# The MLP's second matrix as two nested levels of seven products, its operands formed ahead on GpSimd and streamed from DRAM

## The chip, the cores and the metric

One core of a Trainium2 chip. The metric is the device time of one execution in microseconds; the time before is the median of three runs. Engines by their short names: PE is TensorE (PEld its weight loads), DVE is VectorE, ACT is ScalarE, POOL is GpSimd, SP issues the DMAs. Everything is float32. P = 128 partitions, F = 512 features.

## The reference, cut to what matters

Four sequences of 1024 rows with 512 features run through a graph attention (L0) and then through a conditioned transformer block (L1).

```python
# L0: v is (4, 1024, 512); 20 neighbours, 16 heads of 32; twice (d = 0, 1)
self_feat = concat([v, q_exp]) @ W_self.T + b_self
w   = softmax(where(mask, qh . kh / sqrt(32), NEG) + label_bias)      # over 20 neighbours
out = einsum(w, kv) through Wout per head;  x = v + relu(self_feat + out_0 + out_1)

# L1: c = cond, six vectors per sequence from silu(c) @ W_mod + b_mod
x = x + g_msa * (attention(modulate(layernorm(x))) @ W_out + b_out)   # 16 heads of 64
x = x + g_mlp * (gelu(modulate(layernorm(x)) @ W1 + b1) @ W2 + b2)    # 512 -> 2048 -> 512
```

W2 has 2048 rows and 512 columns. The product `gelu(...) @ W2` over all 4096 rows is what the change touches.

## The kernel before

Order on every engine is the order in which the program emits instructions (`tc.manual_schedule()`); each engine and the queue of SP run their instructions in that order, each waiting for its own inputs.

**Graph attention.** A loop over steps `s` from -4 to 33 handles 32 tiles of 128 rows, software-pipelined: step `s` has the scores of tile `s`, the softmax of tile `s` (`g_soft1` on DVE, `g_soft2` on GpSimd, `g_soft3` on DVE, `g_soft4` = Exp on ACT, `g_soft5` on DVE and GpSimd), the transposes of the weights of tile `s-1` on PE (`g_weightsT`), the mask work of later tiles (`g_mask1` on GpSimd, `g_mask2` on DVE) and loads four tiles ahead. GpSimd's order in a step is: `t + add` (g_soft2), cast and product of the mask (g_mask1), `wts` = weights times reciprocal sum (g_soft5).

**Products in sevens.** A product of two 2x2 block matrices is formed with seven block products instead of eight. `sums_a` and `sums_b` form the sums of blocks (four subtractions or additions each; one of them in place). `seven` issues the products in the order a, c, b, a2, b2, d, b3 into four PSUM banks ma, mb, mc, md, with small steps between them: ACT copies bank a to bank b; ACT keeps c in SBUF (`s5`); DVE writes bank d as b + s5 (`start_d`) ahead of b2; DVE forms the last quarter as b + s5 (`last`) ahead of b3; each finished quarter (i, j) goes to `done`. `with_four` runs them in that order.

**The MLP** comes last, in blocks of 512 rows (`k` = 0 to 7, VB = 4 tiles). For each block:

- The up phase: for `p` = 0 to 3 (2 and 3 for the first block) seven products of W1 with the transposed, modulated rows `hT`; `gelu` on ACT writes the hidden values into `hs[p]` as four groups of blocks, and `up_sums(p)` on DVE forms the hidden values' sums in `hx[p]` (four operations of 128x512).
- The down phase: seven products with W2, each of 2 x 16 matmuls with the hidden values as stationary and 256 columns of W2 as moving operand. W2 lies in SBUF (`w2s`, 4 MB, loaded once) with three sums of its quarters (`w2x`), formed by DVE once.
- `between()`, emitted after the first product of the down phase: `norm_turn` transposes the next block's four normalised tiles (`xl`) in 32x32 blocks on DVE, alternately into `tx["mlp"][:, 5]` and a buffer `s`, and four DMAs per tile carry each result into `hT`; with every second block the gates are spread again (`spread`); then the block's own rows are loaded from `x2d` into `rows2`, whose four buffers (tag `xl`) are those of the tiles just transposed; and GpSimd adds `bias2` to the four of them.
- `modulated()`, after the fourth product: ACT scales and shifts `hT` (`norm_mod`), GpSimd forms the next up phase's sums (`mlp_rows`, four operations of 128x512).
- `dn_done`: each quarter is multiplied with the gate and added to `rows2` on DVE; finished rows are stored to `out`.

The SP queue carries, in the order of emission, the rows for the next block (`norm_load`), the 16 transposing DMAs, the four row loads and the stores.

Of the kernel before, what the change touches and what calls it, by code (L numbers as in the profile page):

```python
# [12 lines left out]
F32 = mybir.dt.float32  # L13
# [28 lines left out]
def cond_block_kernel(  # L42
# [86 lines left out]
    x2d = [tc.dram_tile([P, F], F32, name=f"x2d{i}") for i in range(NTA)]  # L129


    with ExitStack() as gctx:
# [273 lines left out]
        qp = ctx.enter_context(tc.tile_pool(name="qp", bufs=1, side="right", reuse_waits="tile"))  # L406
        xp = ctx.enter_context(tc.tile_pool(name="xp", bufs=1, side="right", reuse_waits="tile"))
# [293 lines left out]
        def up_sums(p):  # L701
            h = [hs[p][:, 2 * k : 2 * k + 2, :] for k in range(4)]
            sums_a(nc.vector, [hx[p][:, k] for k in range(3)], *h)


# [205 lines left out]

        for s in range(-4, NTA + 2):
            do(g_load, s + 4)
# [16 lines left out]
            do(g_mask1, s + 3)  # L930
            do(g_soft3, s)
# [30 lines left out]
            if s == 31:  # L962
                weight_sums(nc.gpsimd, ("v", 0, 0), wv[0, 0], home_ex)
            if s == 25:
                load_qk(0, 0)
                load_v(0, 0)
                load_qk(0, 1)
# [618 lines left out]
    with ExitStack() as mctx:  # L1586
# [12 lines left out]
        w2s = [mp2.tile([P, 4, F], F32, name=f"w2_{k}") for k in range(4)]  # L1599
        for k in (0, 2, 1, 3):  # L1600
            nc.sync.dma_start(w2s[k], w2[k * F : (k + 1) * F, :].rearrange("(c p) f -> p c f", p=P))
        w2x = [mp2.tile([P, 3, 4, HB], F32, name=f"w2x{k}") for k in range(2)]
        for p in range(4):
            hx[p] = mp2.tile([P, 3, 2, HB], F32, name=f"hx{p}")
# [8 lines left out]
        def dn_lhs(which, t, c):  # L1613
            p, q = divmod(c, 2)
            rows = slice(t * P, (t + 1) * P)
            at = {4: 0, 5: 1, 2: 2}.get(which)
            if at is not None:
                return hx[p][:, at, q, rows]
            return hs[p][:, 2 * {0: 0, 1: 1, 6: 2, 3: 3}[which] + q, rows]

        def dn_rhs(which, t, c):
            k, r = divmod(c, 4)
            at = {4: 0, 5: 1, 3: 2}.get(which)
            if at is not None:
                return w2x[k][:, at, r, :]
            h, f = {0: (0, 0), 1: (1, 0), 2: (1, 1), 6: (0, 1)}[which]
            return w2s[2 * h + k][:, r, f * HB : (f + 1) * HB]
# [141 lines left out]
```

## Time and profile before

| what | us |
|---|---|
| median of three runs (lowest to highest) | 3020.31 (3020.05 to 3021.0) |
| the profiled execution | 3032.2 |
| its span, first to last instruction | 3030.2 |
| graph attention, first to last scores (`pa`) | 73.5 to 403.8 of the span |
| attention of L1, first scores (`psc`) to last values (`pav`) | 418.8 to 2263.3 |
| first down phase starts | 2299.7 |
| last product of the last down phase starts | 3018.2 |

The trace's times count from the span's first instruction. The page shows busy time by engine; the windows table shows busy time of each engine in a stretch, then the granted TensorE clock (1.00 is full speed), the mean busy share of the DMA engines and the rate in GB/s; a line of the timeline shows start, duration, engine, line, operation, out<-in, shape and count, and in brackets how long the engine had been idle and who released it. "SPq" lines are the issuing of DMAs, not their transfer.

### The profile page before, as it was taken

What the parts mean: (1) busy time and instruction counts of PE and PEld (TensorE: products, weight loads), DVE (VectorE), ACT (ScalarE), POOL (GpSimd) and SP (SyncE); (2) the same over time, 40 slices, a digit from 0 to 9 for tenths busy, and PEclk for the clock granted to TensorE, in tenths of its full rate; (3) what the DMA queues carried; (4) which work ended last, traced back from release to release, by engine and by line L of the source; (5) the groups of instructions that cost most, each with busy time, mean ns of one, the idle gap of its engine ahead of it and who ended that gap; (6) DMA issues with size and microseconds to landing.
All of it is one profiled execution on the core that took longest, in us unless ns stands there. A gap on an engine that the chain in (4) does not pass through costs nothing.

```text
span 3030.2 us, 41832 instructions
## 1 busy us (share of the span) xinstructions
PE 2995.2 (99%) x15205; PEld 1969.9 (65%) x15205; DVE 2018.4 (67%) x2852; ACT 1441.5 (48%) x2380; POOL 1339.4 (44%) x922
## 2 busy tenths in 40 slices
PE   9999999999999999999999999999999999999999
PEld 6666665565555555555565555555568888888888
DVE  3788867787878877878887878887865332233222
ACT  2344456555755555755555755556641322222211
POOL 1444456555665655665665575664641101110110
PEclk8999999999999999999999999999999999999999
DMA  6343437776877776867776877876764212212020
GB/s 193 118 131 117 136 99 188 167 173 157 204 169 191 191 175 151 209 167 194 190 173 151 206 168 184 198 175 153 190 177 127 49 32 60 56 35 56 29 63 14
DMA packets 341833, 425.25 MB, mean 140 GB/s; under 512 B 88105, under 2 KB 160229, under 8 KB 341629
## 3 DMA queue, kind: packets, MB, share of 16 engines
q1 hardware_dynamic: 341392, 422.37, 55.2%
q8 instruction: 122, 2.00, 0.3%
q14 instruction: 83, 0.67, 0.1%
q10 hardware_dynamic: 236, 0.20, 0.0%
HBM read 120.93 MB, written 25.76 MB: 48 GB/s over the span
## 4 chain that ended last, share of the span: by engine, by line
PE 81%; DVE 7%; POOL 3%; issue 3%; DMA 3%; ACT 2%; SPq 2%; POOLq 0%; DVEq 0%; ACTq 0%
PE q L571 18%; PE psc L1193 14%; PE pav L1101 13%; PE pu L1176 6%; PE mbd L571 5%; PE mbu L571 5%; PE mad L571 4%; PE mau L571 3%; PE mdd L571 2%; PE mcd L571 2%; PE mdu L571 2%; PE mcu L571 2%; DVE mx L1204 1%; DMA wT<-wd 1%; POOL t L780 1%
## 5 line engine op out<-in xcount | busy, mean ns | idle before, releaser
L1219 POOL TENSOR_SCALAR w<-w,sm 128x1024 f32<-128x1024 f32 x256 | 727.8, 2843 | 705.7 <-DVE sm L1215 692.8
L1210 ACT ACTIVATE w<-psc,mx 128x1024 f32<-128x1024 f32 x512 | 570.2, 1114 | 642.8 <-DVE mx L1204 641.6
L1228 DVE STREAM_TRANSPOSE wd<-w 128x1024 f32<-128x1024 f32 x512 | 632.2, 1235 | 110.4 <-ACT w L1217 99.2
L1204 DVE TENSOR_REDUCE mx<-psc 128x1 f32<-128x1024 f32 x512 | 599.3, 1210 | 80.6 <-PE psc L1193 77.4
L1193 PE MATMUL psc<-kT,qT 64*128 64x512 f32 x2048 | 528.0, 615 | 3.6 <-ACT kT L1061 1.4
L1101 PE MATMUL pav<-wT,v 128*64 128x256 f32 x4096 | 482.3, 383 | 2.3 <-DMA wT<-wd 2.0
L1101 PEld LDWEIGHTS pav<-wT,v 128*64 128x64 f32 x4096 | 292.7, 137 | 228.3 <-issue 87.2
L1193 PEld LDWEIGHTS psc<-kT,qT 64*128 64x128 f32 x2048 | 200.2, 186 | 224.0 <-issue 151.4
L1680 POOL TENSOR_TENSOR x<-x,tx 128x512 f32<-128x512 f32 x32 | 39.9, 1279 | 616.9 <-DMA x<-x2d 616.9
L1217 ACT ACTIVATE w<-w,sm 128x1024 f32<-128x1024 f32 x256 | 291.0, 1137 | 0.0
L1185 DVE TENSOR_TENSOR xr<-pu,xr 128x512 f32<-128x512 f32 x210 | 143.6, 684 | 79.7 <-PE pu L1176 79.5
L571 PE MATMUL q<-hT,wqk 128*128 128x512 f32 (+1 forms) x396 | 181.2, 581 | 1.0 <-DVE q L585 1.0
L757 PE MATMUL pa<-kp,sfT 128*128 128x320 f32 x512 | 143.5, 433 | 1.4 <-ACT sfT L732 1.4
L593 ACT COPY mbu<-mau 128x512 f32<-128x512 f32 x30 | 17.1, 570 | 238.9 <-PE mau L571 238.9
L571 PEld LDWEIGHTS q<-hT,wqk 128*128 128x128 f32 x396 | 74.7, 190 | 80.9 <-issue 78.3
L571 PE MATMUL q<-tx,ex 128*128 128x512 f32 (+1 forms) x264 | 123.5, 591 | 1.6 <-POOL tx L656 1.6
L757 PEld LDWEIGHTS pa<-kp,sfT 128*128 128x128 f32 x512 | 94.8, 190 | 38.2 <-ACT sfT L732 1.9
L717 PE MATMUL pf<-wx,xT 128*128 128x512 f32 x256 | 116.0, 597 | 0.0
L571 PE MATMUL mad<-w,hs 128*128 128x256 f32 x512 | 113.1, 379 | 0.0
L571 PEld LDWEIGHTS mad<-w,hs 128*128 128x128 f32 x512 | 97.3, 190 | 13.2
L1176 PE MATMUL pu<-wout,oT 128*128 128x256 f32 x360 | 98.4, 396 | 4.6 <-DVE xr L1185 3.9
L1176 PEld LDWEIGHTS pu<-wout,oT 128*128 128x128 f32 x360 | 62.5, 189 | 59.1 <-issue 31.2
(308 smaller groups left out, 4576.5 us busy)
## 6 DMA issues: line engine op xcount, KB each, us to landing
wT<-wd SPq DMA_DIRECT2D x1024, 256.0 KB
wqk<-in_w_qkv SPq DMA_DIRECT2D x64, 256.0 KB
xT<-in_xt SPq DMA_DIRECT2D x32, 256.0 KB
xs<-in_x SPq DMA_DIRECT2D x32, 256.0 KB
x1d<-xs SPq DMA_DIRECT2D x32, 256.0 KB
xl<-x1d SPq DMA_DIRECT2D x32, 256.0 KB
wv<-in_w_qkv SPq DMA_DIRECT2D x32, 256.0 KB
xr<-x1d SPq DMA_DIRECT2D x32, 256.0 KB
```

The costliest lines, as they stand in the source:

```text
L571: nc.tensor.matmul(t[:, q * width : (q + 1) * width], lhsT=lhs(which, q, k), rhs=rhs(which, q, k), start=(fresh and q == 0 and k == 0), st ...
L717: nc.tensor.matmul(pfs[i], lhsT=xT[i][:, c, :], rhs=wx[:, c, :], start=False, stop=(c == FC - 1), skip_group_check=True,)
L757: nc.tensor.matmul(pas[i][:, n, :HF], lhsT=sfT2[i][:, c, :], rhs=kp[:, b, c, n * HF : (n + 1) * HF], start=False, stop=(c == FC - 1), skip ...
L1101: nc.tensor.matmul(po[j * D : (j + 1) * D, :], lhsT=vt[b, g][:, m, p * P + j * D : p * P + (j + 1) * D], rhs=w[:, j, :, m, :], start=(m == 0),
L1176: nc.tensor.matmul(pu[0][:, q * HB : (q + 1) * HB], lhsT=a[:, q * P : (q + 1) * P], rhs=r, start=(bool(fresh) and q == 0), stop=True, skip ...
L1185: nc.vector.tensor_tensor(o, pu[0].rearrange("p (r f) -> p r f", r=2), o, ALU.add)
L1193: nc.tensor.matmul(sc[j][:, n * F : (n + 1) * F], lhsT=qT[b, gp][q, t * P : (t + 1) * P], rhs=kT[b, gp][q, n * F : (n + 1) * F], start=Tru ...
L1204: nc.vector.tensor_reduce(mx, sc, axis=AX.X, op=ALU.max, negate=True)
L1210: nc.scalar.activation(w, sc, AF.Exp, bias=mx, accum_out=sm)
L1217: nc.scalar.mul(w, w, sm)
L1219: nc.gpsimd.tensor_scalar(w, w, sm, None, ALU.mult)
L1228: nc.vector.transpose(wd[j][:, :, at, :], wn.pop((b, gp, t, j)).rearrange("p (m k) -> p m k", k=U))
```

## The change

W2 is applied as seven products, each of which is again formed by seven: 49 products. For each outer product (`g` counts them, 7 to a block, in the order `ORD` = 0, 4, 1, 5, 6, 2, 3) the stationary operands are 128x128 pieces of the hidden values or sums of them, and the moving operands are 128 columns of W2 or sums of its pieces; an inner product is 4 matmuls.

- **W2's 49 operands** are formed in the graph attention: in four rounds `r` of seven steps (s = -1 to 26) SP loads a quarter of W2 (1 MB) into `w2g` at the end of the round's first step, GpSimd forms the sums in the other six steps (`w2_sum`; two of 128x512 in each of two steps, then one of 128x896 in each of four), emitted between `g_mask1` and `g_soft3`, and SP stores the quarter's 49 pieces (3.2 MB) to `w2d` in DRAM at the end of the last. The buffer takes the place of the pools `qp` and `xp`, which are opened from step 27 on.
- **In the MLP** a ring of three buffers `w2r` takes one outer product's operands (1.84 MB) at a time: `load_w2(g + 2)` is emitted at the start of each outer product, ahead of `between()`.
- **The hidden values' inner sums** (`inner_sums`, four operations of 128x256 for each half `n`) go into `hy[g % 2]`: half 0 on DVE, half 1 on GpSimd, for the next outer product while the present one runs; those of the first outer product of a block and half of the second's are formed by DVE in the up phase.
- `up_sums` loses its fourth operation, which becomes `up_sums4`, run by DVE during the third outer product.
- `inner` has `seven`'s order on the first 128 columns of the four banks, alternating between two sets of banks; a finished quarter goes to one of the accumulators `du`, `d5`, `dv` (ACT copies for outer products 0 and 4, DVE additions for the others).
- `between()` is emitted at the start of the second outer product, without the spreading of the gates, which moves to the start of the down phase; `modulated()` is emitted at the start of the fifth; `finish` multiplies with the gate on DVE and adds to the rows on GpSimd (the last quarter's on DVE).
- The host hands W2 over in another order of its pieces.

```diff
+    w2d = tc.dram_tile([P, 4, 7, 7 * P], F32, name="w2d")
...
-        qp = ctx.enter_context(tc.tile_pool(name="qp", bufs=1, side="right", reuse_waits="tile"))
-        xp = ctx.enter_context(tc.tile_pool(name="xp", bufs=1, side="right", reuse_waits="tile"))
+        gctx2 = ExitStack()
+        tp = gctx2.enter_context(tc.tile_pool(name="tp", bufs=1, side="right", reuse_waits="tile"))
+        w2g = tp.tile([P, 7, 7, P], F32, name="w2g")
...
         def up_sums(p):
-            h = [hs[p][:, 2 * k : 2 * k + 2, :] for k in range(4)]
-            sums_a(nc.vector, [hx[p][:, k] for k in range(3)], *h)
+            a11, _, a21, a22 = (hs[p][:, 2 * k : 2 * k + 2, :] for k in range(4))
+            o1, o2 = (hx[k][:, p] for k in range(2))
+            nc.vector.tensor_tensor(o1, a21, a22, ALU.add)
+            nc.vector.tensor_tensor(o2, o1, a11, ALU.subtract)
+            nc.vector.tensor_tensor(a21, a11, a21, ALU.subtract)
+        def up_sums4(p):
+            nc.vector.tensor_tensor(hx[0][:, p], hs[p][:, 2:4, :], hx[1][:, p], ALU.subtract)
...
+        def w2_load(r):
+            nc.sync.dma_start(w2g[:, :4, :4, :], w2[r])
+        def w2_store(r):
+            nc.sync.dma_start(w2d[:, r], w2g.rearrange("p j i f -> p j (i f)"))
+        def w2_sum(level, n):
+            def at(k):
+                return w2g[:, k, :4, :] if level == 0 else w2g[:, :, k, :]
+            o, i, j = ((4, 1, 0), (5, 3, 4), (1, 3, 1), (6, 2, 5))[n]
+            nc.gpsimd.tensor_tensor(at(o), at(i), at(j), ALU.subtract)
...
         for s in range(-4, NTA + 2):
+            r2, turn2 = divmod(s + 1, 7)
...
             do(g_mask1, s + 3)
+            if 0 <= r2 < 4 and turn2 > 0:
+                for n in ((), (0, 1), (2, 3), (0,), (1,), (2,), (3,))[turn2]:
+                    w2_sum(0 if turn2 < 3 else 1, n)
             do(g_soft3, s)
...
+            if 0 <= r2 < 4 and turn2 == 0:
+                w2_load(r2)
+            if 0 <= r2 < 4 and turn2 == 6:
+                w2_store(r2)
...
-        w2s = [mp2.tile([P, 4, F], F32, name=f"w2_{k}") for k in range(4)]
-        for k in (0, 2, 1, 3):
-            nc.sync.dma_start(w2s[k], w2[k * F : (k + 1) * F, :].rearrange("(c p) f -> p c f", p=P))
-        w2x = [mp2.tile([P, 3, 4, HB], F32, name=f"w2x{k}") for k in range(2)]
+        w2r = [mp2.tile([P, 4, 7, P], F32, name=f"w2r{k}") for k in range(3)]
+        hy = [mp2.tile([P, 4, 2, 2, P], F32, name=f"hy{n}") for n in range(2)]
+        ORD = (0, 4, 1, 5, 6, 2, 3)
+        def load_w2(g):
+            if g < 7 * NB2:
+                at = PLACE[ORD[g % 7]]
+                nc.sync.dma_start(
+                    w2r[g % 3].rearrange("p r i f -> p r (i f)"), w2d[:, :, at]
+                )
...
+        def inner_sums(e, g, n):
+            j = ORD[g % 7]
+            lo, hi = rows_at(j, n), rows_at(j, n + 2)
+            a11, a12, a21, a22 = lo[:, :, :P], hi[:, :, :P], lo[:, :, P:], hi[:, :, P:]
+            o1, o2, o4, o3 = (hy[g % 2][:, k, n] for k in range(4))
+            return [... for o_, x_, y_, op in (
+                    (o1, a21, a22, ALU.add), (o3, a11, a21, ALU.subtract),
+                    (o2, o1, a11, ALU.subtract), (o4, a12, o2, ALU.subtract))]
+        def inner(g, banks, done, room):
...
+            a, b, c, d = (banks[n][:, :P] for n in ("ma", "mb", "mc", "md"))
+            return (
+                (lambda: product(a, 0, True), lambda: nc.scalar.copy(b, a)),
+                (lambda: product(c, 4, True), lambda: nc.scalar.copy(s5, c)),
+                (lambda: product(b, 5), lambda: nc.vector.tensor_tensor(d, b, s5, ALU.add)),
+                (lambda: product(a, 1), lambda: done(0, 0, a)),
+                (lambda: product(b, 6), last),
+                (lambda: product(d, 2), lambda: done(0, 1, d)),
+                (lambda: product(b, 3), lambda: done(1, 0, b)),
+            )
...
+                    if p == 3 and n in (2, 4):
+                        for f in inner_sums(nc.vector, 7 * k, n // 2 - 1):
+                            f()
+                    if p == 3 and n == 2:
+                        for f in inner_sums(nc.gpsimd, 7 * k + 1, 0):
+                            f()
+                if k > 0 or p == 3:
                     up_sums(p)
+                if p == 3:
+                    for f in inner_sums(nc.vector, 7 * k + 1, 1):
+                        f()
...
+            def finish(i, j, y, e=nc.gpsimd):
                 g = gate2[:, j * HB : (j + 1) * HB].unsqueeze(1).to_broadcast([P, 2, HB])
+                nc.vector.tensor_tensor(y, y, g, ALU.mult)
                 for n in range(2):
                     o = rows2[2 * i + n][:, j * HB : (j + 1) * HB]
+                    e.tensor_tensor(o, o, y[:, n], ALU.add)
...
+            for n, which in enumerate(ORD):
+                g = 7 * k + n
+                load_w2(g + 2)
+                if n == 1:
                     between()
+                behind = []
+                if 0 < n < 6:
+                    behind += inner_sums(nc.vector, g + 1, 0)
+                    for f in inner_sums(nc.gpsimd, g + 1, 1):
+                        f()
+                if n == 2:
+                    behind += [lambda p=p: up_sums4(p) for p in range(4)]
+                if n == 3:
+                    behind.append(lambda: finish(0, 0, dv))
+                if n == 4:
+                    nc.gpsimd.tensor_tensor(dv, du, d5, ALU.add)
+                    if nxt < NB2:
+                        modulated()
+                if n == 5:
+                    behind.append(lambda: nc.vector.tensor_tensor(d5, du, d5, ALU.add))
+                if n == 6:
+                    behind += [lambda: finish(0, 1, dv), lambda: finish(1, 1, d5)]
+                done, room = sink(which)
+                steps = inner(g, (dn_banks, up_banks)[n % 2], done, room)
+                for m, (f, after) in enumerate(steps):
+                    f()
+                    after()
+                    for _ in range(-(-len(behind) // (7 - m))):
+                        behind.pop(0)()
+            finish(1, 0, du, nc.vector)
```

## The prediction

> **What bounds the kernel now.** First the page's busy times, then the windows table over one pair of MLP phases, then the timeline of one down phase.
>
> ```profile
> PE 2995.2 (99%) x15205; PEld 1969.9 (65%) x15205; DVE 2018.4 (67%) x2852; ACT 1441.5 (48%) x2380; POOL 1339.4 (44%) x922
> ...
> 2589.98:2638.32 48.34, 48.34 (x225) 42.56 (x224) 10.20 (x19) 4.92 (x8) 9.90 (x8) 1.00 0.25 55
> 2638.32:2686.67 48.35, 48.35 (x225) 42.56 (x224) 17.27 (x28) 17.47 (x38) 0.00 (x0) 1.00 0.10 33
> ```
>
> A down phase (first row: W2 for 512 rows) and an up phase (second row: W1) last 48.35 us each, TensorE without a gap, every other engine mostly idle. There are eight down phases. So TensorE bounds this stage, through the number and width of its matmuls; the others wait at no cost.
>
> ```profile
> 2589.98 7.07 PE L571 MATMUL mad<-w,hs 128*128 128x256 f32 x32
> 2591.86 0.70 DVE L465 STREAM_TRANSPOSE tx<-xl 128x512 f32<-128x512 f32 x1
> 2592.66 2.65 SPq L471 DMA_DIRECT2D hT<-tx  x4
> 2596.88 7.07 PE L571 MATMUL mcd<-w2x,hx 128*128 128x256 f32 x32
> 2597.21 0.71 DVE L465 STREAM_TRANSPOSE tx<-xl 128x512 f32<-128x512 f32 x1 [4.05 <-DMA hT<-tx]
> 2604.50 2.04 SPq L1678 DMA_DIRECT2D x<-x2d  x4
> 2607.39 4.96 POOL L1680 TENSOR_TENSOR x<-x,tx 128x512 f32<-128x512 f32 x4 [83.46 <-DMA x<-x2d]
> 2612.29 1.27 POOL L550 TENSOR_TENSOR tx<-hT 128x512 f32<-128x512 f32 x1
> 2618.60 0.76 DVE L1695 TENSOR_TENSOR x<-x,s 128x256 f32<-128x256 f32 x2
> ```
>
> The reader is to see a long side chain inside the phase: DVE transposes the next block's rows (the third waits 4.05 us for the first one's DMA), SP issues 16 transposing DMAs of 0.66 us, then four row loads, and only then, 17.4 us after the phase began, can GpSimd add the bias to the rows. Today nobody waits for that.
>
> **The change on TensorE.** A product of 32 matmuls of 256 columns takes 6.907 us (2596.88 - 2589.98 = 6.90), 0.216 each. The new phase has 49 products of 4 matmuls of 128 columns.
>
> ```profile
> 416.61 1.28 PE L818 MATMUL po<-vb,wT 128*128 128x128 f32 x10
> ```
>
> Ten of that width take 1.28, and one alone 0.27 (the timeline's row at 414.78): (1.28-0.27)/9 = 0.112 us. 196 x 0.112 = 21.95 us, against 48.35: 26.4 us less a phase if TensorE stayed the bound. I think it doesn't.
>
> **What it now waits for.** I follow a middle phase, t = 0 where TensorE enters it.
>
> Group 0. Before it DVE has up_sums (three adds ending at 1.25) and, new, four 128x256 inner sums at a pitch of 0.34-0.42 (1.45): to 2.7. The product "d" needs DVE's start_d, so group 0 ends near 4.45 and the first transpose starts at 3.95 (before: 1.9).
>
> Row loads. SP's queue now has the 1.84 MB load of group 3's operand ahead of the 16 transposing DMAs; it waits for group 0 to free the buffer.
>
> ```profile
> 2283.00:2290.00 7.00, 7.00 (x34) 6.17 (x33) 5.68 (x9) 3.23 (x8) 0.00 (x0) 1.00 1.05 392
> ```
>
> At the 392 GB/s of the largest loads it takes 4.7 us, from about 6 to 10.7, and the DMAs behind it on the same queue drain after it. So the third transpose starts at about 13.6, not 9.0 (13.6 = 10.7 + 1.9 of data + 1.0 of completion); 5.5 us of issuing follow, then the loads at 19.2, landing 2.9 later as before: R = 22. If the load delays nothing R = 18; if the queue drains slower, 25.
>
> GpSimd's queue. Between the row adds and the next group's operands there is no way round: half of the inner sums of groups 2 to 6 stand behind the four row adds, in order. From R: row adds 4.95; five times four 128x256 operations,
>
> ```profile
> L545 POOL TENSOR_TENSOR osum<-oT,osum 128x256 f32<-128x256 f32 x30 | 21.9, 728 | 0.0
> ```
>
> 2.85 each time at a pitch of 0.70 = 14.25; two 128x256 adds of the first quarter 1.45 (ahead of group 5's sums); dv = du + d5 1.25; mlp_rows 5.0 (both ahead of group 6's sums, which are the last). Sum 26.9, if nothing disturbs it.
>
> Disturbance. DVE and GpSimd hinder one another where both work from SBUF:
>
> ```profile
> 2336.23 1.71 POOL L550 TENSOR_TENSOR hT<-hT 128x512 f32<-128x512 f32 x1
> 2336.92 2.71 DVE L1695 TENSOR_TENSOR x<-x,s 128x256 f32<-128x256 f32 x2
> ```
>
> The pair that took 0.76 alone takes 2.71 beside GpSimd, and GpSimd's 1.27 becomes 1.71. In that stretch DVE has about 13 inner sums (4.4), four up_sums4 (2.4), single 128x128 adds (0.8), three gate products (1.8) and one sum (0.6): 10 us. I charge half, 5, plus 1 for GpSimd's wait on the gate product: 6 (none to 12). The Trainium skill (SBUF — State Buffer, "Who interferes with whom") says that an operation of DVE with two SBUF inputs and one of GpSimd that reads SBUF exclude each other for a whole instruction, "the other fully blocks"; by that all 10 would count, and the sum below would be 7 x 5 = 35 us longer.
>
> After group 6's last sums two products remain: 1 us, or 3 at half clock (1 to 4). TensorE idles 8 us at the third transpose and about 10 more until R + 5.7, and idle time costs clock:
>
> ```profile
> 12.00:17.00 5.00, 3.22 (x29) 3.03 (x28) 1.50 (x5) 2.34 (x3) 0.00 (x0) 1.00 1.01 352
> ...
> 27.00:32.00 5.00, 5.00 (x17) 3.21 (x17) 1.13 (x3) 0.91 (x2) 0.00 (x0) 0.50 1.06 344
> ```
>
> After gaps of about 2 us at 12-17 the granted clock was 0.50 in all three stretches from 17 to 32, some 15 us of interrupted work. I take 3 us there, and 1.7 us at the start of the up phase (half of 3.4 us of work; none to 2). The skill's clock-gate page (TensorE: Matmul & The Clock Gate, Part 1) lets the clock return after about 3.4 us of busy time; by that the last term would be 1 and the sum 14 us shorter.
>
> Phase: 22 + 26.9 + 6 + 3 = 58, and 1.7 later, against 48.35: **+11.3**. Seven phases: +79. By the bounds 18 + 26.9 + 0 + 1 + 0 = 46 (-2.4, or -17 in all) to 25 + 26.9 + 12 + 4 + 2 = 70 (+21.6, or +151).
>
> Last phase: no transposes, no mlp_rows. Row loads go right behind group 3's load, R = 12.5; 12.5 + 21.9 + 6 + 3 = 43.4: **-5** (-14 to +1). First phase: the DVE sums that form W2's operands go (eight of 1.22 us) with TensorE not waiting for them; its new inner sums precede the last product's add: +1 (0 to 3).
>
> Streaming, 56 loads x 4.7 us: three are ahead when a phase starts; groups 5 and 6 are loaded from the ends of groups 2 and 3 (R + 11, R + 18) and needed at R + 23 and R + 33. Nothing; that cover is the GpSimd chain, and without it see the rivals.
>
> **The graph attention.** 24 steps of about 10.5 us get GpSimd sums between its last mask operation and the softmax's scaling: 8 steps two of 128x512 (1.27), 16 steps one of 896 columns (2.47 x 896/1024 = 2.15).
>
> ```profile
> 252.38 0.82 DVE L788 TENSOR_TENSOR t<-t,mx 128x640 f32<-128x640 f32 x1
> 255.47 1.27 POOL L799 TENSOR_TENSOR wts<-t,sm 128x640 f32<-128x640 f32 x1 [3.91 <-DVE sm L797]
> 256.80 0.77 PE L806 MATMUL pt<-ident,wts 128*128 128x128 f32 x5 [0.74 <-POOL wts L799]
> ```
>
> GpSimd's 3.91 us gap would take them, but DVE's subtraction (two SBUF inputs) starts 0.8 us into it. A 2.15 us sum from 251.6, where the last mask operation ends, holds it until 253.75: 1.37 late; two short ones, 0.45. Exp, sum, scaling and TensorE's transposes follow, and TensorE already waits there. 16 x 1.37 + 8 x 0.45 = 25.5; DVE has about 0.45 us a step to spare (15.1 us idle before its 32 first multiplies), 24 x 0.45 = 10.8. Between 14.7 and 25.5 I take **+18** (0 if the sums slip behind the subtraction, 30 with GpSimd's second sum late too). Four stores of 3.2 MB (8.2 us) sit ahead of the next mask loads on SP's queue; those are used some 13 us after issue (202.2 to 215 and later): nothing, a few us if missed.
>
> **Sum.** 79 - 5 + 1 + 18 = +93. The profiled execution took 3032.2 us, its span 3030.2; the runs' median is 3020.3, to which I add the difference: **3113 us**.
>
> **Rivals.**
> A. GpSimd's chain at its floor: R = 18 and DVE's sums fitting into GpSimd's pauses, 46 us a phase. 7 x -2.4 - 14 + 1 + 0..18 = -30 to -12: about 3000. This ends on the other side; it decides where R + 26.9 + the rest falls below 46, two under today. For it: every GpSimd duration is measured. Against: SP's extra load, and the rows of 2.71. Chance 0.10 (0.06 faster, 0.02 equal, 0.02 slower).
> B. TensorE stays the bound (21.95 + 1.3 for group 0: -25 a phase, -200, 2838), or the stream bounds it: 4.45 + 1.3 + 4 x 4.7 + 3.4 = 28, -20 a phase, 2880 with the attention's 18. It needs row adds that don't stand before the sums. 0.04.
> C. The stream is late besides: at half the rate of the big loads (9.4 us each) group 6 lands at R + 18 + 2 + 2 x 9.4 = 61 and the phase ends at 65: with 1.7, +18, 7 x 18 + 19 = +145 and more with a colder clock: 3165 to 3230. For it: rows of 3.5 KB with a stride that no row here shows. 0.10, half of it above my range.
> D. My sum, 3040 to 3165: 0.76.
>
> A measurement of this kernel tells some 0.2% (6 us) from no change. Faster 0.10, same 0.02, slower 0.88. Range **3035 to 3175**: it leaves out B, most of A and half of C.
>
> **What would show it.** In the changed profile: a gap of 8 us or so in TensorE before group 1's "b" products and of some 10 before group 2's; GpSimd's row adds at about 22 us and its busy time unbroken from there to the end of mlp_rows; granted clock under 1 in the down phases; down phases of 55 to 62 us and up phases of 49 to 50; PE waiting for "wts" in the attention, its last step some 18 us later. I am wrong if TensorE is dense in the down phases, or if GpSimd's row adds come before 16 us.

## The result, and the profile after

| | median of the runs, us | lowest to highest | runs |
|---|---|---|---|
| before | 3020.31 | 3017.8 to 3021.34 | 5 |
| after | 3192.75 | 3187.04 to 3197.91 | 5 |

The ratio is 1.0571, with a 95% interval of 1.0555 to 1.0587: 172 us slower. The forecast was 3113 us, with a range of 3035 to 3175. The direction was right, the size was not.

The page of the changed kernel first: busy time, share of the span and instructions of TensorE, VectorE, ScalarE and GpSimd, and the granted clock in forty slices.

```profile
PE 3014.1 (94%) x16549; PEld 2026.9 (63%) x16549; DVE 2213.3 (69%) x3316; ACT 1474.4 (46%) x2524; POOL 1602.2 (50%) x1202
...
PEclk9999999999999999999999999999988988988989
```

TensorE was at 99% and is at 94%, and the last quarter of the span, the MLP, no longer has the full clock. The windows table over one middle block of the MLP (a stretch, then busy time of PE, PEld, DVE, ACT and POOL, the granted clock, the DMA share, GB/s): the first row is a down phase, the second the up phase behind it.

```profile
2555.30:2623.16 67.86, 51.04 (x393) 50.47 (x392) 32.04 (x72) 8.97 (x26) 31.66 (x35) 0.85 0.61 189
2623.16:2671.51 48.35, 48.35 (x226) 42.57 (x225) 20.37 (x34) 17.46 (x38) 3.96 (x4) 1.00 0.26 89
```

The up phase takes 48.35 us as before. The down phase takes 67.86 instead of 48.34. The number in the bracket behind PEld is the most useful one on the page: 392 weight loads for a phase that has 196 matmuls in the program. The timeline of the same phase, TensorE, VectorE and GpSimd (start, duration, operation, shape, records, idle time before and who ended it):

```profile
2562.44 1.06 PE L1694 MATMUL mcu<-w2r,hy 128*128 128x128 f32 x8
2563.33 1.06 PE L1694 MATMUL mbu<-w2r,hy 128*128 128x128 f32 x8
...
2571.77 0.71 DVE L467 STREAM_TRANSPOSE tx<-xl 128x512 f32<-128x512 f32 x1 [10.31 <-DMA hT<-tx]
...
2573.98 2.08 PE L1694 MATMUL mbu<-w2r,hy 128*128 128x128 f32 x8 [8.70 <-DVE mdu L1711]
2575.85 1.92 PE L1694 MATMUL mdu<-w2r,hy 128*128 128x128 f32 x8
2577.56 1.56 PE L1694 MATMUL mbu<-w2r,hx 128*128 128x128 f32 x8
2578.96 1.06 PE L1694 MATMUL mad<-w2r,hs 128*128 128x128 f32 x8
...
2581.06 4.91 POOL L1763 TENSOR_TENSOR x<-x,tx 128x512 f32<-128x512 f32 x4 [33.65 <-DMA x<-x2d]
...
2586.71 1.22 PE L1694 MATMUL mcd<-w2r,hy 128*128 128x128 f32 x4 [6.25 <-POOL hy L1672]
...
2606.31 0.29 DVE L1785 TENSOR_TENSOR du<-mad,du 128x128 f32<-128x128 f32 x1 [1.84 <-POOL dv L1817]
2608.03 1.16 PE L1694 MATMUL mbd<-w2r,hs 128*128 128x128 f32 x8 [1.87 <-DVE s L1705]
```

Three things are to be seen. An inner product, four matmuls in the program, is eight records, and products follow one another every 0.893 us (2563.33 - 2562.44 = 0.89); 49 of them are 43.76 us of TensorE's own work. TensorE stands still three times: for VectorE, which is stuck in front of the third transpose; for GpSimd, whose sums stand behind the row adds; and near the end for VectorE again, which has itself waited 1.84 us for GpSimd's `dv = du + d5`. And behind a wait the products start 1.7 to 1.9 us apart (half clock: 0.50 granted from 2573.98 to 2578.50); behind the first it lasts some 4.6 us (the last of the three slow products took 1.40 instead of 0.89). So 67.86 = 43.76 of work + 16.8 of these three waits + 7.3, nearly all of it half clock.

The whole by the two traces: the first down phase starts at 2325.4 instead of 2299.7 (+25.6); the seven phases with a block behind them take 472.1 us instead of 7 x 48.35 (+133.7); the last takes 54.9 (+6.5). The sum, 165.8, is the difference of the spans but for rounding (3196.1 - 3030.2 = 165.9).

The first of these three numbers is too small. The traced execution of the kernel before granted TensorE only 0.50 of its clock from 17 to 32 us, where all twelve other traces of this case show 1.00; its first mask addition (`t + add`) in the attention comes at 79.0 us, in the others at 68.4 to 70.4, and it took 12 us more than its median. Counted from that addition, the first down phase starts after 2220.7 us in the kernel before and after 2257.0 in the changed one: 36 us later, not 25.6. By the medians it is 172.4 - 133.7 - 6.5 = 32.

### The profile page after: what moved, and what is told of

Read it like the earlier page. It is cut to its first block, busy times and chain, and to the rows that moved or that the text cites. A ratio compares the mean times of both kernels' runs of the same rounds, so it can differ in the third digit from the quotient of the medians.

```text
span 3196.1 us, 45619 instructions
## 1 busy us (share of the span) xinstructions
PE 3014.1 (94%) x16549; PEld 2026.9 (63%) x16549; DVE 2213.3 (69%) x3316; ACT 1474.4 (46%) x2524; POOL 1602.2 (50%) x1202
## 3 DMA queue, kind: packets, MB, share of 16 engines
q1 hardware_dynamic: 371536, 537.98, 62.6%
## 4 chain that ended last, share of the span: by engine, by line
PE 74%; DVE 8%; DMA 5%; POOL 4%; issue 3%; ACT 3%; SPq 3%; POOLq 0%; DVEq 0%; ACTq 0%
PE q L573 17%; PE psc L1226 14%; PE pav L1134 13%; PE pu L1209 5%; PE mbu L573 5%; PE mau L573 3%; PE mbd L1694 3%; SPq L473 2%; PE mdu L573 2%; PE mcu L573 2%; DVE mx L1237 1%; PE mad L1694 1%; ACT w L1243 1%; PE mbu L1694 1%; DMA hT<-tx 1%
## 5 line engine op out<-in xcount | busy, mean ns | idle before, releaser
L1672 POOL TENSOR_TENSOR hy<-hx 128x256 f32<-128x256 f32 x48 | 43.5, 925 | 317.0 <-PE mbu L573 267.7
L1694 PE MATMUL mbu<-w2r,hy 128*128 128x128 f32 x384 | 59.1, 303 | 59.1 <-DVE mdu L1711 59.1
L1243 ACT ACTIVATION_READ_ACCUMULATOR w<-psc,mx 128x1 f32 x512 | 98.6, 193 | 0.0
```

Source lines behind the costliest of these rows:

```text
L1243: nc.scalar.activation(w, sc, AF.Exp, bias=mx, accum_out=sm)
L1694: nc.tensor.matmul(t, lhsT=lhs(which, *divmod(k, 2)), rhs=w2r[g % 3][:, k, PLACE[which], :], start=(fresh and k == 0), stop=(k == 3), skip ...
```

## The experiments

Three questions stood: what is lost ahead of the MLP, what the MLP's waits hang on, and whether my sum failed only in TensorE's own work.

**Attention without the sums.** `w2_sum` is not issued, and the buffer is cleared once, so that W2's sums are left out of the computation.

```diff
         w2g = tp.tile([P, 7, 7, P], F32, name="w2g")
+        nc.gpsimd.memset(w2g, 0.0)
...
-            if 0 <= r2 < 4 and turn2 > 0:
-                for n in ((), (0, 1), (2, 3), (0,), (1,), (2,), (3,))[turn2]:
-                    w2_sum(0 if turn2 < 3 else 1, n)
```

> Leaves out the 24 steps of GpSimd sums that form W2's operands in the graph attention (the array is cleared once instead; its loads and stores and the whole MLP stay), so the output is not the reference's. Theory: GpSimd's sums hold DVE's subtraction, and the loads and stores cost nothing; the first weighted attention then starts near 445 us again (467.1 in the changed kernel, 445.1 before), and the whole is 22 to 25 us shorter: 3168 to 3171. Rival, the four stores of 3.2 MB and loads on SP's queue delay the masks: at most 8 us comes back, 3185 or more.

Measured: 3169.51 us (3169.31 to 3170.54), 23.2 less than the changed kernel. So much do the sums cost, and it is what the theory gave. But they are not all of the loss. The first weighted values come at 443.1 us, and the 445.1 of the kernel before belong to the execution that began 10 us late: counted from the first mask addition, the first down phase starts after 2230.6 us without the sums and after 2220.7 before. Of these 9.9 us, 6.25 lie in one step, behind the first store of 3.2 MB. Without the sums:

```profile
129.31 0.43 SPq L924 DMA_DIRECT2D w2d<-w2g  x1
130.29 1.06 SPq L158 DMA_DIRECT2D xs<-in_x  x1
141.02 0.63 ACT L176 ACTIVATE xs<-xs 128x512 f32<-128x512 f32 x1 [3.48 <-DMA xs<-in_x]
142.06 0.69 PE L893 MATMUL ptm<-ident,mrow 128*128 128x128 f32 x2 [4.52 <-ACT mrow L890]
```

In the kernel before:

```profile
147.56 0.44 PE L885 MATMUL ptm<-ident,mrow 128*128 128x128 f32 x2 [0.95 <-ACT mrow L882]
```

The rows `xs` are queued on SP just behind the store; ScalarE waits for them, its copy `mrow` stands behind that, and TensorE waits for the copy, 4.52 us instead of 0.95. Its next 16 score products then take 6.95 us instead of 4.47. The step is 19.32 us long (from the mask addition at 131.17 to the one at 150.49) instead of 13.07. The other three stores leave no such mark. No run left the store out, so that it is the cause is read from the trace and not shown by an experiment. Another 3.3 us lie between the last weighted values of L1's attention and the first down phase (39.7 us instead of 36.4). The rival was right in part: not the masks but the rows behind the first store were late.

**The same sums in two other places.** First behind the scaling (`g_soft5`):

```diff
             do(g_soft5, s)
+            if 0 <= r2 < 4 and turn2 > 0:
+                for n in ((), (0, 1), (2, 3), (0,), (1,), (2,), (3,))[turn2]:
+                    w2_sum(0 if turn2 < 3 else 1, n)
```

> The same GpSimd sums, put behind the softmax's scaling instead of ahead of the softmax's subtraction. Theory (they cost only where they stand beside DVE's two-input subtraction): most of the 22 us comes back, 15 to 22, so 3171 to 3178. Rival, GpSimd has no room for 2 us more in a step wherever they stand: the next step's mask addition is late instead, and the time stays within 5 us of 3193 or grows.

Then directly behind VectorE's subtraction; a write to one column of the maxima, which the subtraction reads, keeps GpSimd back until it has ended.

```diff
             nc.vector.tensor_tensor(tm, tm, mx.unsqueeze(2).to_broadcast(flat), ALU.subtract)
+            if 0 <= (i + 1) // 7 < 4 and (i + 1) % 7 > 0:
+                nc.gpsimd.memset(mx[:, :1], 0.0)
...
             do(g_soft3, s)
+            if 0 <= r2 < 4 and turn2 > 0:
+                for n in ((), (0, 1), (2, 3), (0,), (1,), (2,), (3,))[turn2]:
+                    w2_sum(0 if turn2 < 3 else 1, n)
```

> The GpSimd sums of the graph attention stand directly behind DVE's subtraction (a one-column write to the maxima that the subtraction read holds GpSimd until it has ended); the MLP is unchanged. Theory (the cost is the overlap with that one subtraction, and between its end and the scaling GpSimd has about 2.2 us free): 16 to 20 of the 23 us come back, 3173 to 3177. Rival (any 2 us more on GpSimd in a step costs, since something of DVE's with two inputs or the next mask operations stand beside it in every slot): no more than 8 us come back, 3185 or more.

Measured: 3201.78 us (3196.24 to 3202.54) behind the scaling, 9 more than the changed kernel; 3175.30 (3173.48 to 3178.46) behind the subtraction, 17.5 less. The timelines of one step tell why. The changed kernel:

```profile
189.48 1.54 POOL L787 TENSOR_TENSOR t<-t,add 128x640 f32<-128x640 f32 x1 [1.36 <-DVE t L777]
192.84 2.08 POOL L931 TENSOR_TENSOR w2g<-w2g 128x896 f32<-128x896 f32 x1
193.71 1.91 DVE L795 TENSOR_TENSOR t<-t,mx 128x640 f32<-128x640 f32 x1
200.50 1.54 POOL L787 TENSOR_TENSOR t<-t,add 128x640 f32<-128x640 f32 x1 [1.36 <-DVE t L777]
```

Behind the scaling:

```profile
203.53 2.54 POOL L931 TENSOR_TENSOR w2g<-w2g 128x896 f32<-128x896 f32 x1
206.03 1.53 POOL L787 TENSOR_TENSOR t<-t,add 128x640 f32<-128x640 f32 x1
```

Behind the subtraction:

```profile
196.14 0.83 DVE L795 TENSOR_TENSOR t<-t,mx 128x640 f32<-128x640 f32 x1
197.03 0.10 POOL L797 MEMSET mx<- 128x1 f32 x1 [1.71 <-DVE t L795]
197.09 2.09 POOL L933 TENSOR_TENSOR w2g<-w2g 128x896 f32<-128x896 f32 x1
199.23 1.27 POOL L808 TENSOR_TENSOR wts<-t,sm 128x640 f32<-128x640 f32 x1
```

In the changed kernel the subtraction starts inside the sum and takes 1.91 instead of 0.83; the step is 11.02 long (200.50 - 189.48). Behind the scaling GpSimd has only the 1.36 that it is idle before the mask addition, the sum needs 2.54 there, and the step is 11.03 again. Behind the subtraction the sum fits into time in which VectorE reduces and takes a reciprocal, and the same trace's mask additions at 191.91 and 201.86 are 9.95 apart, as in the kernel before. The theory of the overlap holds for the original place; for the second place its rival was right, a slot too short. The Trainium skill ("SBUF — State Buffer", "Who interferes with whom") says of such a pair that the second "fully blocks"; this case agrees: the subtraction ends some 0.7 us after the sum does.

**The load behind the transposing DMAs.** On SP's queue the load of group 3's operand moves.

```diff
-                load_w2(g + 2)
-                if n == 1:
-                    between()
+                if n != 1:
+                    load_w2(g + 2)
+                else:
+                    between(g + 2)
...
+                load_w2(g)     # in between(), behind the transposes, ahead of the row loads
```

> Only the load of group 3's weight operand moves on SP's queue: from ahead of the 16 transposing DMAs to behind them, ahead of the row loads. Theory (the 1.84 MB drain ahead of those DMAs): the third transpose starts 7.1 us after the first as in the kernel before, about 12.0 us into the phase instead of 16.5; the wait on it falls from 8.7 to about 4 us; the row adds come later by the load or at the same time as now, so the second wait grows by what the first loses where the row loads are not earlier (R stays near 25) and the phase ends as before: 3180 to 3195. If R falls to 21 as well, each of seven phases ends 4.5 us sooner: 3160. Rival, the transposing DMAs are slow by themselves after the change: the third transpose stays at 16 us and nothing changes.

Measured: 3192.93 us (3185.86 to 3194.68), the changed kernel's time. (The 7.1 us from the first transpose to the third "as in the kernel before" is a misreading: the timeline before has 5.35, 2591.86 to 2597.21.) One middle phase of it, from 2545.89:

```profile
2556.66 0.71 DVE L467 STREAM_TRANSPOSE tx<-xl 128x512 f32<-128x512 f32 x1 [4.60 <-DMA hT<-tx]
...
2558.87 2.08 PE L1694 MATMUL mbu<-w2r,hy 128*128 128x128 f32 x8 [2.99 <-DVE mdu L1711]
...
2571.51 4.92 POOL L1764 TENSOR_TENSOR x<-x,tx 128x512 f32<-128x512 f32 x4 [33.49 <-DMA x<-x2d]
...
2577.16 1.23 PE L1694 MATMUL mcd<-w2r,hy 128*128 128x128 f32 x4 [12.47 <-POOL hy L1672]
```

The third transpose comes 10.8 us into the phase instead of 16.5, so the load did hold the DMAs 5.7 us; it is 5.9 us behind the first transpose. The row adds still start at 25.6, because the load now stands in front of the row loads. The first wait lost 5.7 us, the second gained 6.2: the phase follows the row adds, not the transposes.

**TensorE's work halved.** Two of the four matmuls of each inner product are left out, all sums and DMAs stay.

```diff
-                for k in range(4):
+                for k in (0, 2):
...
-                        stop=(k == 3),
+                        stop=(k == 2),
```

> The changed kernel with two of the four matmuls left out of every product of W2 (one of the two feature chunks of each half), so that TensorE's own work of a down phase is 21.9 us, what my sum on record took for the whole; the output is not the reference's. Everything else, every sum and every DMA, stays. If the rest of that sum is right, a middle phase ends with GpSimd's chain: R + 26.9 + 6 + 3, so 58 us on the record's R of 22, up to 62 with 25.8, and the whole is 3110 to 3150. Rival (the side work hides in the time that TensorE no longer needs): a middle phase loses the whole 21.9 us, 46 us, and the whole is 3017 to 3030.

Measured: 3134.56 us (3133.71 to 3137.78). A middle phase from 2535.49 to 2596.25, TensorE and GpSimd:

```profile
2552.40 1.23 PE L1694 MATMUL mbu<-w2r,hy 128*128 128x128 f32 x4 [9.95 <-DVE mdu L1711]
...
2560.06 4.91 POOL L1763 TENSOR_TENSOR x<-x,tx 128x512 f32<-128x512 f32 x4 [32.46 <-DMA x<-x2d]
...
2565.71 0.80 PE L1694 MATMUL mcd<-w2r,hy 128*128 128x128 f32 x2 [9.10 <-POOL hy L1672]
...
2591.94 1.26 POOL L1672 TENSOR_TENSOR hy<-hs,hy 128x256 f32<-128x256 f32 x1
...
2596.25 1.89 PE L573 MATMUL mau<-hT,wqk 128*128 128x256 f32 x8
```

R, the start of the row adds, is 24.6; GpSimd's last sums end 33.1 us later, the phase 36.2 us later. The record has 33 (26.9 + 6) and 36. With 21.9 us of TensorE work the phase takes 60.8 us: taking half the work away took 7.1 us of 67.9, and the rest of it went into longer waits. The rival, 46 us a phase, falls.

**The row adds later.** On GpSimd's queue they move from ahead of group 2's inner sums to behind group 5's; the sums for the next up phase (`mlp_rows`) go behind group 6's.

```diff
                 if n == 4:
+                    biased()            # the four row adds, out of between()
+                    finish(0, 0, dv)    # was emitted at n == 3
                     nc.gpsimd.tensor_tensor(dv, du, d5, ALU.add)
                     if nxt < NB2:
                         modulated()     # without mlp_rows
                 if n == 5:
+                    if nxt < NB2:
+                        mlp_rows()
```

> On GpSimd's queue the four row adds move from ahead of group 2's inner sums to behind group 5's, and the sums for the next up phase behind group 6's; the rest as in the changed kernel. Theory (TensorE's own work of a phase is 43.8 us, 49 products of 0.893, and all above it is waits and the half clock behind them): the second and third waits go (6.25 and 1.87 us, with about 2.7 and 1.7 us of half clock), the first (8.7 with 2.3) stays, a middle phase takes about 55 instead of 67.9 us, and the whole is 85 to 100 us shorter: 3093 to 3108. Rival, GpSimd's 27 us of work after the row loads sets the end wherever the adds stand: a middle phase stays above 62 us, 3150 or more. Second rival, my sum on record (TensorE's own work 22 us a phase): the phase falls under 45 us, 3030 or less.

Measured: 3152.77 us (3148.17 to 3154.08), 40 us less where 85 to 100 were expected; a middle phase takes 62.6. The second wait went; the third, which was to go as well, grew from 1.87 to 4.14:

```profile
2573.81 5.93 POOL L1765 TENSOR_TENSOR x<-x,tx 128x512 f32<-128x512 f32 x4
2574.32 2.89 DVE L1672 TENSOR_TENSOR hy<-hx 128x256 f32<-128x256 f32 x2
2581.18 1.26 POOL L1818 TENSOR_TENSOR dv<-du,d 128x512 f32<-128x512 f32 x1
2582.47 0.29 DVE L1786 TENSOR_TENSOR du<-mad,du 128x128 f32<-128x128 f32 x1 [3.85 <-POOL dv L1818]
2583.67 2.08 PE L1694 MATMUL mbd<-w2r,hs 128*128 128x128 f32 x8 [4.14 <-DVE s L1705]
```

GpSimd's `dv = du + d5`, for which VectorE had waited 1.84 us in the changed kernel, now stands behind the row adds. VectorE may not write `du` before it has been read, and TensorE's next bank hangs on VectorE. I had moved one thing and not asked who else stands behind it. Beside VectorE the row adds take 5.93 instead of 4.91, and a pair of VectorE sums 2.89 instead of 0.75. The numbers are the first rival's (above 62 us, 3150 or more), but GpSimd's work as such does not set them: the next run keeps it and only orders it otherwise.

**GpSimd's queue in the order of need.** The second quarter gets a place of its own (`dw`, in the buffer that the transposes have left), so `du` comes free early; the row adds and the first quarter's additions go behind group 6's sums.

```diff
+        dw = tx["mlp"][:, 5, :].rearrange("p (t f) -> p t f", t=2)
...
-                o = {0: du, 4: d5, 1: dv, 2: dv}.get(which, du)
+                o = {0: du, 4: d5, 1: dv, 2: dw}.get(which, du)
...
                 if n == 4:
-                    nc.gpsimd.tensor_tensor(dv, du, d5, ALU.add)
+                    nc.gpsimd.tensor_tensor(dw, du, d5, ALU.add)
...
                 if n == 5:
+                    if nxt < NB2:
+                        mlp_rows()
+                    biased()
+                    finish(0, 0, dv, gate=False)
```

> GpSimd's queue ordered by what TensorE needs: the row adds, the first quarter's additions and the sums for the next up phase all behind group 6's inner sums, and dv of the second quarter in a tile of its own, so that nothing overwrites du under DVE. Theory (TensorE's own work of a phase is 43.8 us): only the wait on the third transpose (8.4, with about 2.5 us at half clock) is left, a middle phase takes 54 to 56 us, the whole 3088 to 3110. Rival (DVE and GpSimd hinder one another wherever their work stands): new waits of 4 us and more, a middle phase over 58, 3125 or more. My sum on record, 22 us of TensorE work a phase: under 48 us a phase, 3045 or less.

Measured: 3113.73 us (3109.65 to 3115.92). The windows row of one middle phase:

```profile
2532.00:2589.66 57.66, 47.49 (x393) 46.75 (x392) 37.62 (x72) 8.98 (x26) 30.91 (x32) 0.91 0.72 229
```

The waits left are 8.45 and 1.58 us; 43.76 + 10.0 = 53.8, and 3.9 more, most of it half clock. The phases are 57.4 to 58.3 long where 54 to 56 were expected, and the whole 4 us above its range; no other wait came.

**The third and fourth transposes a group later**, with the row loads behind them (`turned((0, 1))` in group 1, `turned((2, 3))` and `between()` in group 2). The first two transposes also come to stand ahead of group 3's load:

```diff
+                if n == 1:
+                    turned((0, 1))
                 load_w2(g + 2)
-                if n == 1:
+                if n == 2:
+                    turned((2, 3))
                     between()
```

> As the run with the adds last, and the third and fourth transposes with their DMAs and the row loads one group later, behind group 2's operand sums. Theory: no wait over 1.5 us is left in a middle phase, which takes 44 to 47 us, against 48.35 before the change and 67.9 after it: 157 us less over seven, 9 in the last, 3015 to 3045. Rival (the shared access of DVE and GpSimd sets a floor, 35 and 32 us of their work in one phase): 50 us or more a phase, 3060 or more. My sum on record, 22 us of TensorE work: a phase of 35 us or less, 2960 or less.

> The last two edits together: MLP queues in order and the graph attention's sums behind the subtraction. If both theories hold, 16 to 20 us below the run with the MLP's queues alone: 2997 to 3025, at or a little below the kernel before the change. If the attention's loss stays, 3015 to 3045.

Measured: 3087.79 us (3081.82 to 3098.46) with the MLP's edits, 3068.05 (3067.26 to 3070.76) with the attention's sums behind the subtraction as well. The attention's 16 to 20 us came back (19.7), but the MLP's phase is 53.0 to 54.8, not 44 to 47. Neither theory had the cause, a third engine:

```profile
2452.67 2.93 ACT L481 ACTIVATE hT<-hT,modT 128x512 f32<-128x512 f32 x4 [7.08 <-DMA hT<-s]
2455.81 2.07 PE L1695 MATMUL mbd<-w2r,hy 128*128 128x128 f32 x8 [3.91 <-ACT mbd L1710]
```

The transposed rows now arrive later, ScalarE waits for them in front of group 4, and its copy between two banks stands behind that. The numbers are the rival's (50 us or more a phase, 3060 or more), but by luck and not by its mechanism: TensorE waits for ScalarE, and ScalarE for a DMA.

**ScalarE's scaling in group 5**, and the gate products of group 6 behind the fourth inner product:

```diff
                 if n == 5:
                     if nxt < NB2:
+                        behind += [lambda c=c: norm_mod(1, nxt, c) for c in range(FC)]
...
-                    for _ in range(-(-len(behind) // (7 - m))):
+                    for _ in range(-(-len(behind) // (7 - m)) if n < 6 or m > 2 else 0):
```

> As the run with all edits, and two more: ScalarE's four scale-and-shift operations on the transposed rows stand in group 5, between its own copies, instead of ahead of group 4's (3.9 us of wait and about 2.5 at half clock in each of seven phases), and in group 6 the gate products come behind the fourth product (1.6 us). GpSimd's sums for the next up phase and row adds follow in group 6. Theory (TensorE's own 43.8 us a phase and nothing else): a middle phase falls from 53 to 44 to 46 us, 3068 - 7 x 8 = 3012 (3000 to 3025), level with or below the kernel before the change. Rival (GpSimd's work now reaches into the up phase and holds its first sums): waits of 3 us or more at the start of the up phase, 3035 or more.

Measured: 3071.00 us (3064.38 to 3073.52), nothing gained. A row of the waits table (us in total, times, longest) and one of the timeline:

```profile
PE mau L1697 <- DMA w2r<-w2d: 44.5, 11, 6.7
...
2445.57 2.08 PE L1697 MATMUL mau<-w2r,hx 128*128 128x128 f32 x8 [6.29 <-DMA w2r<-w2d]
```

The waits on ScalarE went, and those on VectorE but for 1.3 us, and the stream is late in their place: group 5's load stood in SP's queue behind all 16 transposing DMAs and the row loads. Again neither theory had it; the rival's time (3035 or more) fits, but the waits that it names at the start of the up phase did not come (the up phases take 48.35 us).

**SP's queue in the order of need**: the third transpose in group 2, the fourth in group 3, the row loads in group 4, each behind that group's load.

```diff
                 load_w2(g + 2)
-                if n == 2:
-                    turned((2, 3))
+                if n in (2, 3):
+                    turned((n,))
+                if n == 4:
                     between()
```

> As the run before it with all edits, and SP's queue in the order of need: the third and the fourth transposes, with four DMAs each, stand in groups 2 and 3, the row loads in group 4, each behind that group's operand load; before, the loads of groups 5 and 6 were issued behind all 16 transposing DMAs and the row loads, and TensorE waited 44.5 us for them over the eight phases. Theory (the stream itself is fast enough, 4.7 us a load against 6.25 us of TensorE work a group; only its place in the queue was late): those 44.5 us and about 10 at half clock behind them go, a middle phase takes 44 to 45.5 us, the whole 3005 to 3022, level with the kernel before or up to 0.5% faster. Rival (the transposing DMAs themselves slow the stream, wherever they stand in the queue): 3 us and more of waiting for operands remain in each phase, 3040 or more.

Measured: 3011.00 us (3009.46 to 3013.18, six runs) against 3021.10 (3017.61 to 3025.09, ten runs) of the kernel before beside it: 0.9965, 95% interval 0.9953 to 0.9977. The windows of one block, and the largest sum of TensorE's waits of one kind in the MLP:

```profile
2398.42:2444.11 45.69, 44.35 (x394) 43.96 (x393) 32.88 (x71) 8.98 (x26) 26.00 (x28) 1.00 0.80 258
2444.11:2492.46 48.35, 48.35 (x227) 42.56 (x226) 23.25 (x36) 17.49 (x38) 11.35 (x12) 1.00 0.36 121
...
PE mau L1697 <- DMA w2r<-w2d: 3.5, 5, 1.2
```

A down phase takes 45.69 us at full clock (44.5 to 45.7 over the middle phases): TensorE's 43.76 and no wait over 1.2 us. This is a version that beats both kernels, the one before by 0.35% and the changed one by 5.7%.

## Why the forecast was wrong, and where it was right

**The step that failed: "196 x 0.112 = 21.95 us".** The record says that a product before is "32 matmuls of 256 columns" and that the new phase has "49 products of 4 matmuls of 128 columns". The 32 was counted in records of the trace, the 4 in matmuls of the program, and the price of 0.112 us was one of a record. A float32 matmul leaves two records here: the old product has 16 matmuls in the program (2 x 8, not the 2 x 16 of the description of the kernel before) and 32 records, the new one 4 and 8. The work is 392 x 0.112 = 43.9 us by the record's own price, 43.76 by the trace. So the change takes 4.6 us a phase off TensorE, not 26.4: an eighth of the columns, 6.0 us, less 1.4 because a record of 128 columns costs 0.1116 and one of 256 costs 0.2158. The row I took the price from could have told it: x10 for the five matmuls that its loop issues. The run with half the work puts a price on this step: 3192.75 - 3134.56 = 58 us of the 80 by which the forecast was short.

**R, forecast 22 with bounds of 18 and 25.** It was 25.8 in the changed kernel, 24.6 with half the work. The load held the transposing DMAs 5.7 us, not 4.6. The record has the third transpose at 13.6 us, it came at 16.5: 10.0 us behind the issue of the load (6.4) instead of 7.6. No row shows the record's 1.9 us of data and 1.0 of completion by themselves. The first transpose started at 4.87 in the changed kernel and at 4.05 with half the work, against 3.95 on record: it stands behind group 0's fifth product. At 24.6, R is 2.6 us late in each of seven phases, 18 of the remaining 22 us.

The other terms cancel in part. Ahead of the MLP's first down phase the loss is about 33 us (23.2 for the sums by the medians, 9.9 without them by the traces) against 18 + 1 on record: 14 more. The last phase (below) is 5 more. The 1.7 us that I charged to each up phase, 12 in all, did not come. 58 + 18 + 14 + 5 - 12 = 83, against the 80 by which the forecast was short.

**GpSimd's chain, 26.9 + 6 behind R**, came out right with half the work: 33.1, of which 30.6 are busy and 2.5 idle, so 3.7 us of disturbance and 2.5 of waiting where the record has 5 and 1. **The tail** of 3 us was right there too (36.2 - 33.1). In the changed kernel the sums end at R + 33.8 and the tail is 8.3, since a group needs 6.25 us of TensorE instead of 3.1. That 33.8 is close to 33 is luck: GpSimd is idle for 5.3 us of it, 4.8 of them in one wait for VectorE's gate product, and its busy time is not unbroken, as the record's sign asks.

What a phase waits for is shown by two runs. With the load moved the transposes come 5.7 us earlier and the phase is as long, because the row adds come when they did: up to there GpSimd's queue decides, not the transposes. With half the work GpSimd's chain sets the end. In the changed kernel itself TensorE is the bound again from R + 5.65 on: of the 36.4 us from 2586.71 to the end, 29.9 are its own work (33.5 products), and the rest is the wait of 1.87 and half clock. That is the work which the record had halved.

**The clock.** I took 3 us for half clock at the end and 1.7 at the start of the up phase. The up phase paid nothing (48.35). Inside the phase it was some 7 us, spread over the three waits. Work ran at half clock for 2.8 to 5.5 us after such waits (2.8 behind the 6.29 us in the run with ScalarE's scaling moved, 4.6 behind the 8.70 and 5.5 behind the 6.25 in the changed kernel, 5.4 behind the 12.47 in the run with the load moved), not for the 15 us that I had read off the start of the trace, which only that one execution shows. The rule that the record cites from the Trainium skill's "TensorE: Matmul & The Clock Gate", Part 1, some 3.4 us, is nearer to these.

**The last phase**, forecast -5, came to +6.5, and with half the work to about 0: its row adds wait as well (TensorE 6.17 us for GpSimd's sums), and most of the rest is TensorE's work again.

**The attention**, forecast +18 for the sums, cost 23 for them. The mechanism is the one on record: the subtraction held by a sum that starts ahead of it. It takes 1.08 us longer where a sum of 896 columns stands, and the step is 1.07 longer, so there is no slack of 0.45 a step to set against it, which I had allowed. The stores, forecast at "nothing, a few us if missed", were not nothing: the step behind the first one is 6.25 us longer, through the rows behind it on SP's queue and not through the masks that the record looked at.

**Streaming**, forecast at nothing "and without it see the rivals": nothing in the changed kernel, 44.5 us once GpSimd's chain no longer covered it and group 5's load stood behind the row loads. Rival C gave a time that fits (3165 to 3230) by a mechanism that did not occur: no wait on a load of W2's operands stands among TensorE's larger ones in the changed kernel. Rival B's stream bound of 28 us a phase was never open, with 43.76 us of work.

Where the expected gain is: in the last version seven phases take 23.0 us less than before and the last 3.8 less, out of 8 x 4.6 = 36.7. What stands ahead of the first down phase takes some 14 back (2235.0 us from the first mask addition to the first down phase, against 2220.7): what is left of the sums' cost, the first store, and a wait of 2.15 us for VectorE at the end of the first up phase. 26.8 - 14.3 = 12.5, against 10.1 measured.

## What to carry to other kernels

Count both sides of a comparison in the same unit: divide the records of a row by the matmuls that its loop issues before a price per record is multiplied by a number read from code. Where a change fills idle time of in-order engines, one wait removed uncovers the next one (GpSimd, then VectorE, then ScalarE, then SP here), so the order of every queue has to follow the order in which the bottleneck needs its inputs. Count a stage from its own first instruction, not from the start of the trace: one execution can begin 10 us late. And an engine's idle gap is room only if it is as long as the new piece and nothing that shares its SBUF access is due inside it.

## What the runs showed of the hardware that was not expected

- A wait of 1.57 or 1.58 us left the clock alone (the three products behind it came at full pace in the runs with the adds last and with both edits). Of the seven waits of 1.86 to 1.97 us in the changed kernel, six were followed by about 1.7 us of loss, the first by none; in the run with the load moved three of seven were followed by none. So the length of the wait does not decide alone. The loss can begin one product after the wait: in the changed kernel products start at 2608.03, 2609.03, 2610.45 and 2612.16, so 1.0, 1.4 and 1.7 us apart. What else decides, and whether earlier waits count, was not tried.
- SP's queue is held by a large load even for the DMAs that do not need it: with the 1.84 MB load ahead of them, the first four transposing DMAs took 3.96 us to issue in the changed kernel (2.65 before, 3.02 with the load behind them, 7.88 for the third transpose's four behind the loads of groups 3 and 4 in the run with ScalarE's scaling moved).
- The 2.1 us between the end of VectorE's subtraction and that of its reciprocal hold a GpSimd sum of 2.09 us at no cost to that step (9.95 us with and without it). VectorE's operations there have one input each; the subtraction, which a sum did hold, has two.
